# Conv block and attention: the gate, pointwise and feed-forward banks emptied by copies, with silu and GELU applied once over each whole tile

## The chip, the cores and the metric

The kernel runs on one core of one Trainium2 chip. The metric is device time in microseconds. Five engines work on one core, each through its own queue in order: PE (TensorE: matrix products and transposes; its weight loads are shown as PEld), DVE (VectorE), ACT (ScalarE), POOL (GpSimd) and SP (SyncE, which issues DMAs here). [...]

## The reference, cut to what matters

Everything is float32. The input is four pictures of 64 x 64 points with 256 channels. The first layer mixes a small state-space scan, a depthwise convolution and a feed-forward part; the second layer is attention over all 4096 points of a picture.

```python
# layer 1, h = layernorm(x)
x_proj, z = split(h @ in_proj_W)                      # 384 channels each
dt  = silu(proj @ dt_W + dt_b)                        # forward and backward
y_ssm = scan over 2x2 windows with exp(dt * a), 8 states, both directions
y_conv = gelu(depthwise3x3(x_proj) @ pw_W)            # exact GELU
y = alpha * y_ssm + (1 - alpha) * y_conv
x_out = x + (y * silu(z)) @ out_W
fuse = gelu(layernorm(x_out) @ fuse_W1 + fuse_b1) @ fuse_W2 + fuse_b2
x = x_out + fuse
# layer 2
attn = softmax(g @ f.T);  out = gamma * ((attn @ hh) @ Wo + bo) + x
```

## The kernel before, in words

The first layer goes through 32 blocks of 512 points (8 rows of a picture; 8 blocks a picture). Channels stand on the 128 partitions, the 512 points along the row; 384 channels are KI = 3 chunks, the 512 hidden channels of the feed-forward part KF = 4. A generator, `first_layer`, writes out the work of the blocks. `scan(at)` makes the decays (Exp, L406), lets PE turn them into PSUM banks (L462) and lets DVE step the states (L470, L474, L492, L485). Beside it runs `side(at)`, which does the rest of the block before: `conv` (depthwise; products at L574, the other taps on DVE at L595), `gate`, `tail`, and the `head` of the next block. `prepare` makes dt by Silu (L389). Each `yield` names a cost in us, and by these costs the pieces are interleaved.

After the eighth block attention begins. `attend` runs over 128 queries at a time; `weights` makes their scores (L844), copies them out of four banks (L852), takes the maximum on DVE (L858, L860), subtracts it (L877) and takes Exp (L878); L1036 adds up the values. While it runs, `fill(RATE)` draws pieces of the first layer of later pictures. When the first layer is done, `attend_late`, `late_weights` and L1014, L935 do the remaining queries, 256 at a time.

The order so written is the input of a scheduler in the framework, which gives each engine its own list of instructions from its own estimates; a later step puts a table load ahead of each ACT function that the current table doesn't hold. So a program that is built can be listed, engine by engine, and these lists are fixed at run time.

Small products go to PSUM banks from `aside`, a ring of four banks q0 to q3, which the scores use whole (`four`); the scan has a ring of three others (`bank`).

The change touches three places, each of which fills a tile chunk by chunk from such banks:

- `gate`, L342 and L346: three products for z, each emptied by Silu with a bias into a chunk of `zs` (128 x 3 x 512).
- `tail`, L626 and L631: three pointwise products, each emptied by two GELU instructions of 256 columns (they also permute the points) into `yz`. Then, on DVE, L639 and L642 mix in the scan and the gate, and L649 multiplies by out_W; L653 adds the input.
- `tail`, L669 and L673: four products with fuse_W1, each emptied by GELU with a bias into a chunk of `ff` (128 x 4 x 512). L680 multiplies by fuse_W2, L684 adds on DVE. Then come transposes (L312, copied out at L313) and the inputs of attention (L693, L704), stored by SP.

`zs`, `yz` and `ff` have one buffer each; the buffers of `yz` and `ff` are used again in the same block (h2T and vst; ydw and xT).

Of the kernel before, what the change touches and what calls it, by code (L numbers as in the profile page):

```python
# [22 lines left out]
AF = mybir.ActivationFunctionType  # L23
# [11 lines left out]
KI = INNER // P  # L35
# [24 lines left out]
def block_then_attention_kernel(  # L60
# [18 lines left out]
    nc = tc.nc  # L79
# [28 lines left out]
    def load_rows(dst, at):  # L108
        b, i = divmod(at, NBLK)
        for t2 in range(2):  # L110
            for wr in range(ROWS // 2):
                nc.sync.dma_start(
                    out=dst[wr * 32 : (wr + 1) * 32, 2 * t2 : 2 * t2 + 2, :].rearrange("p t c -> p (t c)"),
                    in_=xv[b, i, t2, wr],
                )

    def load_head(at):
        xt = one.tile([P, 4, DIM], F32, tag="norm", name="xt")
        load_rows(xt, at)
        heads[at] = xt  # L120
# [55 lines left out]
    def aside(shape=(P, TOK)):  # L176

        i = turn[0]
        turn[0] = (i + 1) % 4
        return pss.tile(list(shape), F32, tag=f"q{i}", name=f"q{i}")  # L180
# [9 lines left out]
    b_in = wp.tile([P, 2 * KI], F32, name="b_in")  # L190
    b_f1 = wp.tile([P, KF], F32, name="b_f1")
# [98 lines left out]
    def layernorm(dst, src):  # L290

        stats = st.tile([P, 4, 6], F32, tag="stats", name="stats")
        mv = st.tile([P, 4, 2], F32, tag="mv", name="mv")
        for t in range(4):
            nc.vector.bn_stats(stats[:, t, :], src[:, t, :])
        for t in range(4):
            nc.vector.bn_aggr(mv[:, t, :], stats[:, t, :])
        ve = st.tile([P, 4], F32, tag="ve", name="ve")
        rstd = st.tile([P, 4], F32, tag="rstd", name="rstd")
        nc.gpsimd.tensor_scalar(ve, mv[:, :, 1], EPS, None, ALU.add)  # L300
        nc.gpsimd.tensor_tensor(rstd, ve, mhalf, ALU.pow)
        for t in range(4):
            nc.vector.tensor_scalar(
                dst[:, t, :], src[:, t, :], mv[:, t, 0:1], rstd[:, t : t + 1], ALU.subtract, ALU.mult
            )

    def to_channels(dst, src):

        for k in range(KD):
            pt = aside()  # L310
            for t in range(4):
                nc.tensor.transpose(pt[:, t * P : (t + 1) * P], src[:, t, k * P : (k + 1) * P], ident)  # L312
            nc.scalar.copy(dst[:, k, :], pt)  # L313
            yield 0.44
# [21 lines left out]
    def gate(at, whole):  # L336
        xnT = heads[at][0]
        zs = one.tile([P, KI, TOK], F32, tag="zs", name="zs")
        for f in range(KI):
            pz = aside()  # L340
            for k in range(KD):
                nc.tensor.matmul(  # L342
                    pz, lhsT=win[:, k, INNER + f * P : INNER + (f + 1) * P], rhs=xnT[:, k, :],
                    start=(k == 0), stop=(k == KD - 1),
                )
            nc.scalar.activation(zs[:, f, :], pz, AF.Silu, bias=b_in[:, KI + f : KI + f + 1])  # L346
            if not whole:
                yield 1.72
        gates[at] = zs
        if whole:  # L350
            yield 5.2

    def prepare(at):
# [41 lines left out]
        if at < NBLK:  # L395
            yield 3.3
            if at > 0:
                yield from gate(at - 1, True)
# [216 lines left out]
    def tail(at):  # L615

        b, i = divmod(at, NBLK)
        zs, s, ydw = gates.pop(at), heads.pop(at)[1], ydws.pop(at)
        xo = one.tile([P, 4, DIM], F32, tag="xo", name="xo")
        load_rows(xo, at)  # L620

        yz = one.tile([P, KI, TOK], F32, tag="yz", name="yz")
        for f in range(KI):
            pw = aside()
            for k in range(KI):
                nc.tensor.matmul(  # L626
                    pw, lhsT=wpw[:, k, f * P : (f + 1) * P], rhs=ydw[:, k, :],
                    start=(k == 0), stop=(k == KI - 1),
                )
            for t2 in range(2):  # L630
                nc.scalar.activation(  # L631
                    yz[:, f, t2 * 256 : (t2 + 1) * 256].rearrange("p (t1 wr wc) -> p t1 wr wc", t1=2, wr=ROWS // 2),
                    pw.rearrange("p (wr t2 wc t1) -> p t2 t1 wr wc", wr=ROWS // 2, t2=2, t1=2)[:, t2],
                    AF.Gelu,
                )
            yield 2.58

        for f in range(KI):
            nc.vector.scalar_tensor_tensor(  # L639
                yz[:, f, :], yz[:, f, :], one_a[:, f : f + 1], s[:, f, :], ALU.mult, ALU.add  # L640
            )
            nc.vector.tensor_tensor(yz[:, f, :], yz[:, f, :], zs[:, f, :], ALU.mult)  # L642
            yield 1.3
        for t2 in range(2):
            po = aside((P, 2, DIM))
            for t1 in range(2):
                t = 2 * t2 + t1
                for k in range(KI):
                    nc.tensor.matmul(  # L649
                        po[:, t1, :], lhsT=yz[:, k, t * P : (t + 1) * P], rhs=wout[:, k, :],  # L650
                        start=(k == 0), stop=(k == KI - 1),
                    )
            nc.vector.tensor_tensor(xo[:, 2 * t2 : 2 * t2 + 2, :], po, xo[:, 2 * t2 : 2 * t2 + 2, :], ALU.add)  # L653
            yield 3.2

        h2 = one.tile([P, 4, DIM], F32, tag="norm", name="h2")
        layernorm(h2, xo)
        yield 5.0
        for t in range(4):
            nc.gpsimd.tensor_tensor(xo[:, t, :], xo[:, t, :], row, ALU.add)  # L660
        h2T = one.tile([P, KD, TOK], F32, tag="yz", name="h2T")
        yield from to_channels(h2T, h2)
        if at + 3 < LAST:
            load_head(at + 3)
        ff = one.tile([P, KF, TOK], F32, tag="ff", name="ff")
        for f in range(KF):
            pf = aside()
            for k in range(KD):
                nc.tensor.matmul(  # L669
                    pf, lhsT=wf1[:, k, f * P : (f + 1) * P], rhs=h2T[:, k, :],  # L670
                    start=(k == 0), stop=(k == KD - 1),
                )
            nc.scalar.activation(ff[:, f, :], pf, AF.Gelu, bias=b_f1[:, f : f + 1])  # L673
            yield 1.72
        for t2 in range(2):
            pq = aside((P, 2, DIM))
            for t1 in range(2):
                t = 2 * t2 + t1
                for k in range(KF):
                    nc.tensor.matmul(  # L680
                        pq[:, t1, :], lhsT=ff[:, k, t * P : (t + 1) * P], rhs=wf2[:, k, :],
                        start=(k == 0), stop=(k == KF - 1),
                    )
            nc.vector.tensor_tensor(xo[:, 2 * t2 : 2 * t2 + 2, :], pq, xo[:, 2 * t2 : 2 * t2 + 2, :], ALU.add)  # L684
            yield 4.0
        nc.sync.dma_start(out=x1d[at], in_=xo.rearrange("p t c -> p (t c)"))
        yield 0.0

        xT = one.tile([P, KD, TOK], F32, tag="ff", name="xT")
        yield from to_channels(xT, xo)  # L690
        pf = aside()
        for k in range(KD):
            nc.tensor.matmul(pf, lhsT=wfg[:, k, :], rhs=xT[:, k, :], start=(k == 0), stop=(k == KD - 1))  # L693
        fg = two.tile([P, TOK], F32, tag="uT", name="fg")
        nc.scalar.activation(fg, pf, AF.Identity, bias=b_fg)
        nc.sync.dma_start(out=fgd[at], in_=fg)
        yield 1.72

        vst = one.tile([P, 4, DIM + 1], F32, tag="yz", name="vst")
        nc.gpsimd.memset(vst[:, :, DIM : DIM + 1], 1.0)  # L700
        for t in range(4):
            po = aside()
            for k in range(KD):
                nc.tensor.matmul(  # L704
                    po[:, :DIM], lhsT=xT[:, k, t * P : (t + 1) * P], rhs=wv[:, k, :],
                    start=(k == 0), stop=(k == KD - 1),
                )
            nc.vector.tensor_tensor(vst[:, t, :DIM], po[:, :DIM], bv, ALU.add)
            yield 1.2
        nc.sync.dma_start(out=vod[at], in_=vst.rearrange("p t c -> p (t c)"))  # L710
# [35 lines left out]
    def first_layer():  # L746
# [44 lines left out]
        yield from drain("tail", LAST - 2)  # L791
        yield from conv(LAST - 1)
        yield from gate(LAST - 1, False)
        yield from tail(LAST - 1)
        ready["tail"] = LAST - 1

# [392 lines left out]
```

## Time and profile before

| | us |
|---|---|
| median of 3 runs (5250.38 to 5259.54) | 5259.01 |
| the profiled execution's own time | 5265.47 |
| its span | 5263.6 |
| PE busy | 4955.8 (94%) |
| DVE busy | 4517.3 (86%) |
| ACT busy | 3571.5 (68%) |
| ACT table loads, 643 of 1.283 us | 825 |
| POOL busy | 204.0 (4%) |

The profile is of one execution. Busy shares are averages over three stretches with different limits: up to about 880 us the first layer of the first picture runs alone, up to about 4270 us the first layer of the other pictures runs beside attention, and the rest is attention alone. An engine's idle time is put down to whoever released it: "PE q L844 <- ACT zs L346" says that PE stood before a score product into a bank q until ACT had emptied that bank into zs. PE shown as busy includes the modelled ends of pipelined products; PEld shows the weight loads, which run ahead of them.

### The profile page before, as it was taken

How to read it: one execution, taken by the hardware profiler on the slowest of the kernel's cores; microseconds unless marked ns; L12 is line 12 of the kernel's file. 1: busy time of each engine (PE TensorE's matmuls, PEld its weight loads, DVE VectorE, ACT ScalarE, POOL GpSimd, SP SyncE). 2: the span in 40 equal slices, each digit the busy share in tenths (PEclk: the TensorE clock that was granted, in tenths of full speed). 3: DMA queues.
4: the chain of work that ended last, by engine and by line, in shares of the span. 5: the costliest groups of instructions: out<-in, count | busy, mean ns of one | idle time of the engine just before them, and what ended most of it. 6: DMA issues, size and time to landing. Idle time of an engine off the chain costs nothing. (4 is left out here: it accounts for less than half of the span.)

```text
span 5263.6 us, 76327 instructions
## 1 busy us (share of the span) xinstructions
PE 4955.8 (94%) x27138; PEld 3543.4 (67%) x27138; DVE 4517.3 (86%) x8256; ACT 3571.5 (68%) x5489; POOL 204.0 (4%) x304
## 2 busy tenths in 40 slices
PE   7999998999999999999999999999999999999999
PEld 4565565666666666666666666666666667888887
DVE  7999999999899988998989988898989866666665
ACT  6778778667777767677777767777777635555554
POOL 0000000000000000000000000000000000000000
PEclk8999999999999999999999999999999999999999
DMA  1010011333333333334333333333333344444444
GB/s 48 26 44 19 23 34 34 102 122 115 118 104 119 113 109 115 114 116 118 118 111 106 119 108 111 118 114 118 112 116 104 112 129 146 147 147 147 147 147 139
DMA packets 330284, 554.14 MB, mean 105 GB/s; under 512 B 51504, under 2 KB 85936, under 8 KB 329904
## 3 DMA queue, kind: packets, MB, share of 16 engines
q1 hardware_dynamic: 326384, 545.40, 34.2%
q8 instruction: 214, 3.51, 0.3%
q10 hardware_dynamic: 3520, 3.87, 0.2%
q14 instruction: 166, 1.36, 0.1%
HBM read 490.28 MB, written 58.79 MB: 104 GB/s over the span
## 5 line engine op out<-in xcount | busy, mean ns | idle before, releaser
L1036 PE MATMUL acc<-vt,eq 128*128 128x257 f32 x4736 | 1215.4, 392 | 17.2 <-issue 7.6
L406 ACT ACTIVATE e<-dt,a_sc 128x384 f32<-128x384 f32 x1536 | 853.3, 611 | 272.8 <-PE bank L462 262.5
L1036 PEld LDWEIGHTS acc<-vt,eq 128*128 128x128 f32 x4736 | 875.0, 195 | 234.2 <-issue 107.6
L462 PEld LDWEIGHTS bank<-ident,e 128*128 128x128 f32 x4320 | 521.2, 143 | 319.5 <-issue 113.4
L462 PE MATMUL bank<-ident,e 128*128 128x128 f32 x4320 | 658.9, 279 | 79.1 <-DVE p L474 37.1
L1014 PE MATMUL bank<-vt,eT 128*128 128x257 f32 x2560 | 645.8, 382 | 0.0
L492 DVE SCALAR_TENSOR_TENSOR h<-u,bc,p 128x384 f32<-128x384 f32 x1024 | 613.4, 613 | 0.4
L485 DVE SCALAR_TENSOR_TENSOR y<-h,bc,y 128x384 f32<-128x384 f32 x960 | 589.0, 614 | 3.2 <-ACT y L483 0.4
L474 DVE TENSOR_TENSOR p<-bank,h 128x384 f32<-128x384 f32 x960 | 517.1, 548 | 55.1 <-PE bank L462 54.5
L1014 PEld LDWEIGHTS bank<-vt,eT 128*128 128x128 f32 x2560 | 478.6, 189 | 83.7 <-issue 13.9
L852 ACT COPY eq<-q 128x512 f32<-128x512 f32 x592 | 308.6, 587 | 192.6 <-PE q L844 117.5
L948 DVE TENSOR_TENSOR mx<-mx,eT 128x512 f32<-128x512 f32 x378 | 261.7, 692 | 152.2 <-ACT eT L943 121.3
L878 ACT ACTIVATE eq<-eq 128x1024 f32<-128x1024 f32 x296 | 308.1, 1053 | 103.0 <-DVE eq L877 100.1
L877 DVE TENSOR_TENSOR eq<-eq,nb 128x1024 f32<-128x1024 f32 x296 | 357.4, 1220 | 7.6 <-ACT nb L873 7.4
L595 DVE SCALAR_TENSOR_TENSOR ydw<-xp,vec,ydw 128x512 f32<-128x512 f32 x496 | 357.8, 743 | 1.4
L943 ACT COPY eT<-q 128x512 f32<-128x512 f32 x432 | 221.5, 597 | 194.7 <-PE q L935 194.7
L860 DVE TENSOR_TENSOR mx<-mx,eq 128x512 f32<-128x512 f32 x444 | 306.5, 690 | 38.4 <-ACT eq L852 31.5
L406 ACT ACT_TABLE_LOAD x241 | 309.2, 1283 | 14.4 <-PE bank L462 10.2
L485 DVE SCALAR_TENSOR_TENSOR y<-p,bc,y 128x384 f32<-128x384 f32 x512 | 313.1, 612 | 0.4
L470 DVE SCALAR_TENSOR_TENSOR p<-bank,bc,u 128x384 f32<-128x384 f32 x480 | 291.6, 608 | 21.1 <-PE bank L462 20.6
L973 DVE TENSOR_TENSOR eT<-eT,m 128x1024 f32<-128x1024 f32 x216 | 247.7, 1219 | 42.3 <-ACT m L970 42.3
L626 PE MATMUL q<-ydw,wpw 128*128 128x512 f32 x576 | 269.5, 602 | 13.3 <-ACT eq L852 12.8
(154 smaller groups left out, 7524.7 us busy)
## 6 DMA issues: line engine op xcount, KB each, us to landing
vt<-vod SPq DMA_DIRECT2D x1616, 257.0 KB, 2.8
vod<-vst SPq DMA_DIRECT2D x32, 514.0 KB, 3.9
xt<-in_x_dram SPq DMA_DIRECT2D x256, 64.0 KB, 1.9
xo<-in_x_dram SPq DMA_DIRECT2D x256, 64.0 KB, 2.3
x1d<-xo SPq DMA_DIRECT2D x32, 512.0 KB, 2.9
res<-x1d SPq DMA_DIRECT2D x74, 128.0 KB, 2.6
out_dram<-res SPq DMA_DIRECT2D x296, 32.0 KB, 1.6
fgd<-fg SPq DMA_DIRECT2D x32, 256.0 KB, 2.1
```

What stands on the lines that cost most here:

```text
L406: nc.scalar.activation(e[:, f, :], dts[d][:, f, lo : lo + 3 * P], AF.Exp, scale=a_sc[:, d, f * NST + n : f * NST + n + 1],)
L462: nc.tensor.transpose(pa[:, f * P : (f + 1) * P], es[d, n][:, f, off : off + P], ident)
L474: nc.vector.tensor_tensor(p, pa[:, :INNER], hs[d], ALU.mult)
L485: nc.vector.scalar_tensor_tensor(y[:, t, :], h, c, y[:, t, :], ALU.mult, ALU.add)
L492: nc.vector.scalar_tensor_tensor(hs[d], u[d][:, t, :], bc[:, t, d, n : n + 1], p, ALU.mult, ALU.add)
L595: nc.vector.scalar_tensor_tensor(o, x_tap, w_tap, o, ALU.mult, ALU.add)
L852: nc.scalar.copy(e[:, j, :], pr[2 * a + j])
L860: nc.vector.tensor_tensor(mx, mx, e[:, r % 2, :], ALU.max)
L877: nc.vector.tensor_tensor(e8, e8, nb.unsqueeze(1).broadcast_to([P, 8, P]), ALU.add)
L878: nc.scalar.activation(e, e, AF.Exp)
L1014: nc.tensor.matmul(sums[c][:, : DIM + 1], lhsT=e[:, r % 2, s, c * P : (c + 1) * P], rhs=vt[:, s, :], start=(n == 0 and s == 0), stop=(n == ...
L1036: nc.tensor.matmul(acc[:, : DIM + 1], lhsT=es[k // 2][:, k % 2, a : a + P], rhs=vt[:, s, :], start=(n == 0 and s == 0), stop=(n == 2 * NI ...
```

## The change

Each bank is emptied by a copy: Identity with the same bias (zs, ff) or Copy with the same permutation (yz). When the tile is full, one instruction applies Silu or GELU in place over the whole tile: 1536 elements a partition for zs and yz, 2048 for ff. In `gate`, when it runs piece by piece, the wide Silu stands after the last piece's yield; in `tail` the wide GELU stands after the last yield of its loop. The other activations (dt at L389, the Exps) stay as they are. From L349 on, lines move down by one, from L638 by two, from L677 by three.

```diff
@@ gate
-            nc.scalar.activation(zs[:, f, :], pz, AF.Silu, bias=b_in[:, KI + f : KI + f + 1])
+            nc.scalar.activation(zs[:, f, :], pz, AF.Identity, bias=b_in[:, KI + f : KI + f + 1])
             if not whole:
                 yield 1.72
+        nc.scalar.activation(zs, zs, AF.Silu)
         gates[at] = zs
@@ tail
                 nc.scalar.activation(
                     yz[:, f, t2 * 256 : (t2 + 1) * 256].rearrange("p (t1 wr wc) -> p t1 wr wc", t1=2, wr=ROWS // 2),
                     pw.rearrange("p (wr t2 wc t1) -> p t2 t1 wr wc", wr=ROWS // 2, t2=2, t1=2)[:, t2],
-                    AF.Gelu,
+                    AF.Copy,
                 )
             yield 2.58
+        nc.scalar.activation(yz, yz, AF.Gelu)
@@ tail
-            nc.scalar.activation(ff[:, f, :], pf, AF.Gelu, bias=b_f1[:, f : f + 1])
+            nc.scalar.activation(ff[:, f, :], pf, AF.Identity, bias=b_f1[:, f : f + 1])
             yield 1.72
+        nc.scalar.activation(ff, ff, AF.Gelu)
         for t2 in range(2):
```

## The prediction

> **What bounds the kernel now.** I read the busy shares first, then the three stretches of the span, then who waits for whom in the middle one, then the ACT groups. The page's busy line, and the stretches "first layer alone" (0 to 880 us), "first layer beside attention" (to 4270), a short end of it, and "attention alone" (columns: PE, PEld, DVE, ACT, POOL busy us, then clock, DMA share, GB/s):
>
> ```profile
> PE 4955.8 (94%) x27138; PEld 3543.4 (67%) x27138; DVE 4517.3 (86%) x8256; ACT 3571.5 (68%) x5489; POOL 204.0 (4%) x304
> ...
> 0.00:880.00 880.00, 812.58 (x3508) 500.14 (x3508) 830.25 (x1704) 662.88 (x1059) 55.15 (x87) 0.97 0.10 32
> 880.00:4270.00 3390.00, 3162.15 (x17983) 2251.29 (x17983) 3066.38 (x5661) 2422.52 (x3716) 144.59 (x210) 0.97 0.37 113
> 4270.00:4345.00 75.00, 69.95 (x348) 48.95 (x347) 35.17 (x58) 32.46 (x48) 4.29 (x7) 0.98 0.43 128
> 4345.00:5263.00 918.00, 911.13 (x5304) 743.01 (x5302) 585.46 (x836) 453.62 (x669) 0.00 (x0) 1.00 0.49 146
> ```
>
> ACT is the engine that the change touches, and it is never the fullest. Alone, the first layer is paced by DVE (830 of 880 us; 244 of 250 between 250 and 500 us). Beside attention PE is busy 93% and DVE 90% and each waits for the other; ACT is busy 71%. The last 918 us hold none of the changed lines. So at most the idle time that ACT causes on PE and DVE before 4270 us can be won. The lists of waits of the middle stretch, PE's, PEld's and DVE's (us in total, times, longest):
>
> ```profile
> PE q L342 <- ACT eq L852: 20.8, 14, 2.7
> PE q L626 <- ACT eq L852: 12.8, 8, 2.2
> ...
> PE q L844 <- ACT zs L346: 8.2, 10, 2.5
> ...
> PE q L844 <- ACT yz L631: 5.2, 6, 1.6
> ...
> PE q L844 <- ACT ff L673: 1.2, 4, 0.5
> ```
> ```profile
> PEld q L844 <- ACT zs L346: 19.6, 24, 2.7
> ...
> PEld q L844 <- ACT yz L631: 11.2, 19, 1.8
> ```
> ```profile
> DVE mx L860 <- ACT eq L852: 29.4, 28, 2.1
> ...
> DVE mx L858 <- ACT eq L852: 19.5, 18, 2.4
> ...
> DVE yz L639 <- ACT yz L631: 3.7, 3, 2.6
> ```
>
> Adding the whole lists by releaser: ACT ends 105 us of PE idle (75.5 of it the score copies L852, 14.6 the three banks zs, yz, ff) and 60 us of DVE idle (49 of it L852). DVE ends 108 us of PE idle, PE 198 us of DVE idle. Last, what ACT does at the changed lines:
>
> ```profile
> L406 ACT ACT_TABLE_LOAD x241 | 309.2, 1283 | 14.4 <-PE bank L462 10.2
> ...
> L631 ACT ACT_TABLE_LOAD x86 | 110.3, 1283 | 28.0 <-issue 21.5 <-PE q L626 5.5
> L673 ACT ACT_TABLE_LOAD x83 | 106.5, 1283 | 1.4
> ...
> L346 ACT ACT_TABLE_LOAD x79 | 101.4, 1283 | 1.3
> L878 ACT ACT_TABLE_LOAD x77 | 98.8, 1283 | 2.1 <-DVE eq L877 0.9
> L389 ACT ACT_TABLE_LOAD x75 | 96.2, 1283 | 1.3
> ```
>
> With two at the start these are 643 loads, 825 us: 23% of ACT's busy time, most of them because a silu or a GELU stands between two groups of Exp.
>
> **What the Trainium skill says.** All from the page "ScalarE: Activation LUTs". "Table sets: the hidden batching unit" says that copy and identity are in every set. The trace agrees: L331, L423 and L852 (Identity and copies) have no load row. "Step-by-step: what each stage is for" says that time per element does not depend on the function: L331 (Identity, bias) takes 685 ns, L346 (Silu, bias) 687, both 128x512. "What ACT_TABLE_LOAD costs" gives 1283 ns a load plus a drain of about 1380. The load is 1283 here too; of the drain I see nothing: at 431.99 us an Exp ends, at 432.01 the load starts, it ends at 433.29 and the GELU starts at 433.30. I price a load at 1.28 us.
>
> **The change part by part.**
>
> Copies for functions: 96 Silu, 192 GELU of 256 columns and 128 GELU of 512 become Identity or Copy. By the 685/687 pair this costs nothing on ACT, within 35 ns for the 192 Copies (L563, a Copy, takes 721 against 685): at most 7 us of ACT time, which has 29% of slack.
>
> Loads removed: in the built order of the changed program I count 346 loads instead of 643. The three lines keep 32 each (one per block, at the wide instruction), the Exp lines fall from 241 to 141 (L406) and from 77 to 31 (L878), dt goes from 75 to 76. 297 x 1.283 = 381 us less on ACT. Beside attention a block of 141 us has 21.6 loads before and 10.9 after; alone it has 16 and 10.
>
> Wide instructions added: the 128x1024 Exp L878 takes 1053 ns; less 1024 x 0.833 ns (that page's price per element) 200 ns are fixed. So 1536 elements take about 1.48 us (64 of them, zs and yz) and 2048 about 1.91 us (32, ff): 95 + 61 = 156 us. Net on ACT: -381 + 156 = **-225 us**, 8.8 us of a block's 101 beside attention, 2.8 us alone.
>
> What of it reaches the span. *Alone*: nothing; DVE has 2.4% idle there, and 3 us of it is ACT's. *Beside attention*: the banks are emptied without a load ahead of the copy. Of the 14.6 us that PE waited for them I take 10. L852's copies are late when ACT comes from a load, but not when all four ring banks are simply full: four copies of 0.59 us need 2.3 us whatever happens, and ACT itself stood waiting for the scores in 86 of 148 groups (49 times for L844, 37 for L1036), so it was on time there. I take a third of 75.5 us on PE, 25, and 3 of the 9 us at e and dt. Together **-38 us** on PE; the bounds are 0 and 105. DVE's third of 49 us lies inside this, since the two run in step.
>
> What is made later. The first product of fuse_W2 (L680, after: L683) needs the whole ff: last copy 0.69, load 1.28, GELU 1.91, 3.9 us in all, where before the last bank alone was awaited (0.69, and 1.28 if a load stood there). Nothing of ff is ready earlier, so the early products cannot be slipped in. Between the last product into ff and the first out of it the built order puts other PE work: I summed it with issue intervals of the timeline (0.43 us for 512 columns, 0.215 for 257, 0.135 for a 128-column transpose). Beside attention it was 2.2 us a block and becomes 3.1: most often two groups of L462 transposes, L327 x2 and L1036 x4, 2.5 us. In 19 of the 24 blocks beside attention it is short, 24 us in sum. For yz the need is copies 0.7, load 1.28, GELU 1.48 and three DVE steps, 5.6 us; the PE work in between is 2.8 before and 4.0 after; short by 37 us in sum, against 23 us before (need 3.4: the last bank 0.66, a load, two DVE steps). Of those 23 the trace shows 3.5 us as PE idle and 10.2 as PEld idle at L649: the rest is hidden, since PE comes to such places late. Taking these shares, 15 to 45%, of 24 + 37 - 23 = 38 us gives +6 to **+17**; I take 12. DVE's own wait is covered: its first step on yz, L639, was placed level with the transposes that precede the last product, and is now two or more p steps later, about 3.4 us, what the wide GELU needs. In the alone stretch PE's work in between is paced by DVE, so the wait costs nothing there. If that cover failed, it would be 1 to 2 us a block.
>
> zs is used later than it is made; its wide Silu delays only what is queued behind it on ACT (4.0 us with its loads, against 3.3 for one bank with its loads before). PE's score products then wait at most this 0.8 us a block more, 19 us in the worst case, priced in the range. DMAs, POOL and SP keep their instructions; the x1d, fgd and vod writes come a few us later in a block that is used a picture later, so nothing waits.
>
> Sum: -38 + 12 = **-26 us**. On the profiled execution (span 5263.6, its time 5265.47) that gives 5239; the median of the runs, 5259.01, is 6.5 us lower, so I forecast **5233 us**. About 0.2%, 10.5 us, is what a measurement can tell from no change.
>
> **Rivals.** *Slower: the gathered GELU stalls PE.* In-order PE stands at L683 and at the yz products behind a load and 1.9 or 1.5 us of GELU that no built order hides, since the order does not know the load. It decides if PE arrives on time rather than late: then the shortfall of 38 us is paid in full, with up to 19 us from ACT's longer blocks, and the gain falls to the 10 us of the banks plus some 10 of L852: 5259 + 38 + 10 - 20 = about 5285. For it: less ACT delay makes PE earlier, so the hiding shrinks. Against: 3.5 us of 23 was visible before.
> *Nothing: ACT is not the bound.* DVE and PE wait for each other (108 and 198 us) and take the freed time back: 5259, give or take 10.
> *Far faster.* ACT's backlog is behind nearly all of the 105 us on PE, and part of what PE makes DVE wait for (L684 behind L680, 58 us): 5160 to 5190.
> *The loads don't go.* The built order excludes it.
>
> **How the numbers follow.** Gain as worked out, 5210 to 5247: 0.55. Far faster: 0.10. Nothing: 0.13. Slower: 0.22. So faster 0.65, same 0.13, slower 0.22. The range 5185 to 5280 leaves out the lower half of the far case and the upper half of the slow one.
>
> **What would show it.** Right: ACT busy near 3345 us with 346 loads; the waits of L844 for zs, yz and ff gone; L852 releasing some 50 us of PE idle instead of 75; L683 waiting for the wide ff with 5 to 15 us in sum. Wrong: over 25 us at L683 and L651 for ff and yz (slower rival); or ACT's releases halved while DVE's 108 us on PE grow as much (nothing); or DVE in the alone stretch waiting for yz by over 1 us a block.

## The result, and the profile after

The changed kernel takes 5283.31 us in the median of 4 runs (5280.97 to 5286.2), the kernel before 5258.53: 1.0051 times as long, with a 95% interval of 1.0039 to 1.0064. It is **slower by 25 us**, where 26 us of gain were forecast. The profiled execution took 5280.97 us.

From the page of the kernel after, the busy line:

```profile
PE 4960.2 (94%) x27138; PEld 3542.4 (67%) x27138; DVE 4518.3 (86%) x8256; ACT 3332.3 (63%) x5288; POOL 208.2 (4%) x304
```

ACT lost 239 us of busy time (forecast 225); PE's and DVE's busy time stayed. The groups of the loads and of the wide instructions:

```profile
L407 ACT ACT_TABLE_LOAD x141 | 180.9, 1283 | 2.4
...
L677 ACT ACTIVATE ff<-ff 128x2048 f32<-128x2048 f32 x32 | 61.2, 1912 | 0.4
...
L638 ACT ACTIVATE yz<-yz 128x1536 f32<-128x1536 f32 x32 | 47.5, 1485 | 0.4
```

Counts and durations are those of the forecast (1.91 us for ff, 1.48 for yz, and for zs as for yz). So the question is where the time was lost. The first score product (L844, after: L847) starts at 867.9 us before and at 893.9 after; the first product of attention alone at 4359.7 and 4376.8. Cut at these points, the two stretches after are (us, then PE, PEld, DVE, ACT, POOL busy):

```profile
0.00:893.90 893.90, 809.71 (x3442) 499.27 (x3442) 822.24 (x1687) 622.91 (x1018) 58.97 (x89) 0.96 0.10 31
893.90:4376.80 3482.90, 3254.57 (x18475) 2311.27 (x18474) 3122.42 (x5753) 2263.02 (x3614) 149.21 (x215) 0.98 0.38 114
```

The first layer **alone is 26.0 us longer**, the stretch beside attention 8.9 us shorter (3491.8 before). All of the loss lies where "nothing" was forecast. The gain beside attention is no more than the difference between executions: the profiled one of before took 7 us more than the median of its runs, that of after 2 us less.

Alone, the blocks repeat themselves, so one block can be laid beside another, from one copy of proj (L361, after: L362) to the next. A block before, and two blocks after:

```profile
294.58:389.34 94.76, 90.64 (x398) 56.02 (x397) 92.67 (x188) 73.74 (x119) 6.15 (x9) 1.00 0.10 32
```
```profile
499.83:597.67 97.84, 91.15 (x398) 56.08 (x397) 93.08 (x188) 70.56 (x115) 6.56 (x9) 1.00 0.08 25
399.73:499.83 100.10, 93.70 (x398) 58.15 (x397) 93.06 (x188) 70.54 (x115) 6.55 (x9) 0.97 0.08 28
```

Before, a block takes 94.75 us each time. After, it takes 97.84 where TensorE's granted clock is 1.00, and up to 100.1 where short dips of the clock bring its mean down to 0.97. What DVE waits for in the block of 97.84 us:

```profile
DVE h L303 <- POOL rstd L301: 1.2, 1, 1.2
DVE xt L303 <- POOL rstd L301: 1.2, 1, 1.2
DVE p L475 <- PE bank L463: 0.6, 1, 0.6
DVE p L471 <- PE bank L463: 0.5, 1, 0.5
DVE xo L687 <- PE q L683: 0.4, 1, 0.4
DVE vst L711 <- PE q L707: 0.4, 1, 0.4
DVE y L486 <- ACT y L484: 0.2, 1, 0.2
```

Before, the same list has three lines and 1.7 us: the first one here, 0.3 at L708 and 0.2 at L419. After it is 4.5 us. The second line is the largest new one, and it isn't about a changed tile: in the head's layernorm, POOL makes 1/sigma. DVE's order around it after, with the idle time in brackets:

```profile
311.69 0.24 DVE L297 BATCH_NORM_AGGREGATE mv<-stats 128x2 f32<-128x6 f32 x2
311.85 0.72 DVE L596 SCALAR_TENSOR_TENSOR ydw<-xp,vec,ydw 128x512 f32<-128x512 f32 x1
313.81 0.41 DVE L303 TENSOR_SCALAR xt<-xt,mv,rstd 128x256 f32<-128x256 f32 x1 [1.24 <-POOL rstd L301]
```

One row (one DVE instruction) stands between the last aggregate and the normalise that needs POOL's answer. Before, eleven rows stand there (L470 to L485, from 316.88 to 323.05), and there is no wait:

```profile
316.72 0.24 DVE L297 BATCH_NORM_AGGREGATE mv<-stats 128x2 f32<-128x6 f32 x2
...
323.05 0.41 DVE L303 TENSOR_SCALAR xt<-xt,mv,rstd 128x256 f32<-128x256 f32 x1
```

So the built order is another one here, though no instruction of the head was edited. (The expectations below say nine rows: they count lines of the view, two of which hold two rows.)

In the whole stretch DVE's idle time grew by 22 us and its busy time by 4. By releaser the idle time is: 7.4 us more for POOL at xt; 6.6 more for transposed decays (L471, L475); 9.2 more at the two adds behind the products with yz and ff (L655, L687). Other waits fell by a little over 1 us.

Beside attention, PE's waits that the forecast named, after:

```profile
PE q L342 <- ACT eq L855: 17.2, 11, 2.7
...
PE q L651 <- DVE yz L644: 10.0, 10, 2.4
...
PE q L847 <- ACT yz L632: 3.1, 2, 1.5
...
PE q L847 <- ACT zs L346: 2.1, 4, 0.9
```

All that ACT releases on PE there fell from 105.5 to 80.3 us, L852's share (after: L855) from 75.7 to 61.7. What DVE releases rose from 114 to 129 us, and 10.0 us of that are a wait that the list of before doesn't have: the products with yz (L651). In all, PE's waits fell by 8 us, from 230.7 to 222.8.

### The profile page after: what moved, and what is told of

Its sections match the earlier page's. It is cut to its first block, busy times and chain, and to the rows that moved or that the text cites. A ratio compares the mean times of both kernels' runs of the same rounds, so it can differ in the third digit from the quotient of the medians.

```text
span 5279.1 us, 75983 instructions
## 1 busy us (share of the span) xinstructions
PE 4960.2 (94%) x27138; PEld 3542.4 (67%) x27138; DVE 4518.3 (86%) x8256; ACT 3332.3 (63%) x5288; POOL 208.2 (4%) x304
## 5 line engine op out<-in xcount | busy, mean ns | idle before, releaser
L475 DVE TENSOR_TENSOR p<-bank,h 128x384 f32<-128x384 f32 x960 | 516.7, 547 | 47.9 <-PE bank L463 47.2
L855 ACT COPY eq<-q 128x512 f32<-128x512 f32 x592 | 309.4, 590 | 220.9 <-PE q L847 141.5
L471 DVE SCALAR_TENSOR_TENSOR p<-bank,bc,u 128x384 f32<-128x384 f32 x480 | 291.5, 607 | 23.5 <-PE bank L463 23.1
L1017 PE MATMUL acc<-vt,eT 128*128 128x257 f32 x896 | 272.2, 386 | 0.0
```

Source lines behind the costliest of these rows:

```text
L475: nc.vector.tensor_tensor(p, pa[:, :INNER], hs[d], ALU.mult)
L855: nc.scalar.copy(e[:, j, :], pr[2 * a + j])
L1017: nc.tensor.matmul(sums[c][:, : DIM + 1], lhsT=e[:, r % 2, s, c * P : (c + 1) * P], rhs=vt[:, s, :], start=(n == 0 and s == 0), stop=(n == ...
```

## The experiments

Times are medians; the ratio to the kernel before, run on the same chip, stands with its interval. "Alone" is the time until the first score product and "beside" the time from there to attention alone, both from one profile of each kernel (runs of the kernel before alone lie 16 us apart, so small differences between these columns prove nothing). "Block" is the period of a block alone, or the range of six periods where it varies by over 1 us.

| kernel | us | ratio | alone | beside | block |
|---|---|---|---|---|---|
| before | 5258.53 | | 867.9 | 3491.8 | 94.75 |
| after | 5283.31 | 1.0051 (1.0039 to 1.0064) | 893.9 | 3482.9 | 97.84 to 100.13 |
| zs only | 5235.44 | 0.9950 (0.9935 to 0.9965) | 863.5 | 3463.3 | 94.70 |
| yz only | 5301.06 | 1.0077 (1.0062 to 1.0092) | 887.7 | 3509.1 | 96.95 to 99.29 |
| ff only | 5281.17 | 1.0038 (1.0023 to 1.0052) | 887.4 | 3488.1 | 97.69 to 99.39 |
| as before alone, as after beside | 5258.04 | 0.9998 (0.9989 to 1.0006) | 865.6 | 3488.4 | 94.76 |
| after, functions left out | 5229.01 | 0.9944 (0.9929 to 0.9958) | 876.0 | 3450.4 | 95.45 |
| before, functions left out | 5193.85 | 0.9873 (0.9857 to 0.9890) | 862.6 | 3429.3 | 94.22 |
| after, head without POOL's answer | 5281.86 | 1.0044 (1.0029 to 1.0059) | 885.5 | 3491.0 | 96.74 to 98.97 |
| zs, and ff beside only | 5241.24 | 0.9966 (0.9953 to 0.9979) | 864.6 | 3473.5 | 94.70 |
| ff in halves | 5260.21 | 1.0005 (0.9996 to 1.0014) | 879.1 | 3475.9 | 96.46 |
| zs, ff in halves | 5242.04 | 0.9969 (0.9957 to 0.9981) | 875.9 | 3460.6 | 96.40 |
| yz only, GELU left out | 5268.81 | 1.0023 (1.0013 to 1.0033) | 869.4 | 3496.5 | 95.56 |

**The parts one by one.** Each kernel takes one of the three edits of the diff and leaves the others. *zs only*:

```diff
-            nc.scalar.activation(zs[:, f, :], pz, AF.Silu, bias=...)
+            nc.scalar.activation(zs[:, f, :], pz, AF.Identity, bias=...)
...
+        nc.scalar.activation(zs, zs, AF.Silu)
```

> Only gate is changed (copies into zs, one wide Silu); yz and ff as before; 545 loads. In the profiles a block of the first layer alone takes 94.75 us before and 98.9 after, and this makes the whole loss. Theory 'late results' (yz and ff come later than the work that DVE and PE have in between): zs is not urgent, so a block alone stays at 94.8 to 95.8 us, and the kernel takes 5245 to 5262. Rival 'long ACT stops' (any wide instruction between two loads holds up the Exps behind it): a third of the loss, 96 us a block, about 5267. Rival 'the scheduler's order' (any edit gives a new order of about equal badness): 97 to 99 us a block, about 5280.

Measured: 94.70 us a block, and 26 us faster in all (5261.33 for before in these runs). "Late results" foresaw the block; the total is better than it foresaw. The list of DVE's waits in a block is that of before, with the same three times (1.2, 0.3 and 0.2 us). So a wide instruction between two loads need not do harm, and an edit need not bring a bad order.

Where do the 26 us come from? The stretch beside attention, first before, then with the gate edit:

```profile
867.90:4359.70 3491.80, 3255.81 (x18476) 2315.50 (x18475) 3125.37 (x5761) 2468.51 (x3785) 148.88 (x217) 0.98 0.37 113
863.50:4326.80 3463.30, 3227.03 (x18475) 2295.64 (x18474) 3123.84 (x5761) 2383.27 (x3718) 150.55 (x217) 0.98 0.38 114
```

The stretch is 28.5 us shorter, and PE's busy time (first number behind the comma) is 28.8 us shorter for the same products; PE's waits are the same, 230.7 and 231.2 us in sum. By the clock records of the two traces the mean granted clock in this stretch was 0.975 before and 0.984 here, and 3255.8 x 0.975 / 0.984 is about 3226. So in these profiles the gain beside attention is a higher clock and no shorter wait. All four runs of this kernel had a mean clock of 0.983 or 0.984.

*yz only*:

```diff
-                    AF.Gelu,
+                    AF.Copy,
...
+        nc.scalar.activation(yz, yz, AF.Gelu)
```

> Only the pointwise banks are changed (copies into yz, one wide GELU); 540 loads. 'Late results': DVE waits are small at yz but PE's L649 and what follows come later: 95.5 to 97 us a block alone, 5262 to 5275. 'Long ACT stops': 96 us, about 5267. 'Order': 97 to 99 us, about 5280.

Measured: the worst of all, mostly 98.8 to 99.3 us a block and 17 us more beside. A block's window, three of the first four of DVE's waits in it, and what PE waited for most there:

```profile
592.72:691.47 98.75, 93.24 (x398) 58.11 (x397) 93.23 (x188) 69.99 (x115) 6.62 (x9) 0.97 0.08 25
```
```profile
DVE xt L303 <- POOL rstd L301: 1.2, 1, 1.2
...
DVE xo L654 <- PE q L650: 0.9, 1, 0.9
DVE xo L685 <- PE q L681: 0.9, 1, 0.9
```
```profile
PE pa L462 <- ACT e L406: 1.4, 1, 1.4
PE bank L462 <- DVE p L470: 1.2, 1, 1.2
```

The same POOL wait as in the kernel after; 0.9 us at the add behind the products with yz, and 0.9 at the next add, where PE comes late; and a clock of 0.97. The block is what "order" named and longer than "late results" named; the total is above every expectation.

PE does not come late because it waits for yz: no wait for yz stands in its list of this block. It waits 1.4 us for the decays `e`. On ACT a load, the wide GELU and the load back stand in front of that Exp, from 639.56 to 643.65 us, 4.1 us in one piece. (Before, PE's waits for `e` in a block are at most 0.2 us each.) Together with the 1.2 us for DVE just ahead of it, PE was busy 1.17 of the 3.41 us before 643.92; then the clock was 0.50 for the next 3.4 us, in which the products with yz begin. So "long ACT stops", which zs only seemed to exclude, is what the trace shows here, though it had named 96 us: what matters is whether an Exp that PE needs stands behind the stop. The kernel after has the same 1.4 us wait in each of its six regular blocks.

*ff only*:

```diff
-            nc.scalar.activation(ff[:, f, :], pf, AF.Gelu, bias=...)
+            nc.scalar.activation(ff[:, f, :], pf, AF.Identity, bias=...)
...
+        nc.scalar.activation(ff, ff, AF.Gelu)
```

> Only the feed-forward banks are changed (copies into ff, one wide GELU of 2048); 541 loads. In the profile after, DVE waits 1.5 us a block at the add of the fuse_W2 product for PE, which waited for the wide GELU. 'Late results': those 1.5 us or a little more, 96 to 97.5 us a block alone, 5265 to 5278. 'Long ACT stops': 96 us, about 5267. 'Order': 97 to 99 us, about 5280.

Measured: 97.69 us at full clock; DVE waits 1.2 us for POOL at xt, 1.3 for transposed decays and 0.6 at L685. Block and total are those of "order", a little above "late results". The three parts do not add: alone +20 (yz), +19.5 (ff) and -4 (zs), but +26 together. Each of the two slow parts brings the same POOL wait, which is paid once: some 9 us in the stretch, about what the sum is off.

**Where the loss lies.**

```diff
+        if at >= NBLK:
+            nc.scalar.activation(zs, zs, AF.Silu)        # yz and ff in the same way
```

> Blocks 0 to 7 (the first layer alone) as before, blocks 8 to 31 (beside attention) as after. If the loss lies in the alone stretch (+26 us until the first scores in the profiles) and the stretch beside attention gained 9 us: the first scores at 868 us as before, and 5240 to 5255, faster than both. If the loss lies beside attention, or the gain there is only the noise of one profile: 5258 to 5283.

Measured: the first scores at 865.6 us, so the alone stretch is as before, and the total is that of before (0.9998). The loss is the alone stretch. The gain beside is only 3 us in this profile, against 9 after: nothing that can be told from the spread of the runs.

**Load or lateness.**

```diff
-        nc.scalar.activation(yz, yz, AF.Gelu)
+        nc.scalar.activation(yz, yz, AF.Copy)           # Identity for zs and ff
```

> As after, but the three wide instructions apply Identity or Copy: silu and GELU are left out, so that the wide instructions stay as long and as late while their table loads go (154 loads left). At full clock a block alone takes 94.75 us before and about 97.9 after. If the cost is how late the wide results come (0.69 + 1.91 us for ff even without a load), 96 to 97.5 us a block; if the load in front of the wide instruction is what makes it too late, 94.5 to 95.3. Beside attention: shorter than after by 5 to 30 us.

Measured: 95.45 us, between the two ranges and nearer to that of the load. DVE's longest waits in a block of it:

```profile
DVE h L303 <- POOL rstd L301: 1.2, 1, 1.2
DVE xo L687 <- PE q L683: 0.7, 1, 0.7
DVE p L475 <- PE bank L463: 0.6, 1, 0.6
...
```

The POOL wait at xt is gone, since in this built order six rows stand at that place. That is 1.2 of the 2.4 us that a block is shorter than after; PE's wait for `e` is down from 1.4 to 0.5 us. As the order changed with the loads, the two are not taken apart here. Beside attention the stretch is 32 us shorter than after: 23 us less waiting of PE and 9 us less busy time. The other half of the pair takes the functions out of the kernel before:

```diff
-            nc.scalar.activation(ff[:, f, :], pf, AF.Gelu, bias=...)
+            nc.scalar.activation(ff[:, f, :], pf, AF.Identity, bias=...)   # zs too; Copy for yz
```

> As before, but the three banks are emptied by Identity or Copy and silu and GELU are left out: no wide instruction, 154 loads. A block alone 94.3 to 94.8 us (DVE paces it, so loads cost nothing there). Beside attention it bounds what all the removed loads could bring: if ACT's backlog mattered as the forecast took it, 40 us or more below before's 3492; if only the granted clock and the order move that stretch, within 20 us of it.

Measured: 94.22 us a block, as expected (DVE paces it; without functions it is 0.5 shorter). Beside, it is 62 us less than before. That stretch, here and with the wide instructions without functions:

```profile
862.60:4291.90 3429.30, 3227.43 (x18478) 2300.36 (x18477) 3120.27 (x5763) 1970.83 (x3398) 152.33 (x217) 0.98 0.38 115
876.00:4326.40 3450.40, 3245.20 (x18475) 2311.24 (x18474) 3120.74 (x5753) 2077.86 (x3470) 149.24 (x215) 0.98 0.38 115
```

Of the 62 us, 28 are shorter PE busy time (3255.8 to 3227.4, the clock again) and 34 are shorter waits of PE (230.7 to 197.0): somewhat less than the 40 us that the forecast's view of ACT's backlog asked for. Between the two kernels without functions a block alone differs by 1.2 us (95.45 and 94.22). Beside, they differ by 21 us, but 18 of these are PE busy time, and PE's waits are 199.6 and 197.0 us. So wide instructions without loads cost PE next to no waiting there. The kernel after has 192 loads more than these two, and there PE waits 23 us more than with wide instructions without functions, 21 of them behind ACT. So it is the loads that are left, and not the wide instructions as such, that go with the small gain.

**The wait for POOL.**

```diff
-                dst[:, t, :], src[:, t, :], mv[:, t, 0:1], rstd[:, t : t + 1], ALU.subtract, ALU.mult
+                dst[:, t, :], src[:, t, :], mv[:, t, 0:1],
+                mv[:, t, 1:2] if dst is src else rstd[:, t : t + 1], ALU.subtract, ALU.mult
```

> As after, but the head's layernorm multiplies by the variance in place of the 1/sigma that POOL makes: DVE no longer waits for POOL there. Before, nine DVE rows stood between the last aggregate and the first normalise and hid POOL's 1.25 us; after, one row does. If that new order is a part of the loss of its own: 1.2 us less a block alone (96.6 at full clock), 8 to 10 us less until the first scores. If the wait only takes the place of another one: no change, 97.9.

Measured: 96.74 us at full clock, 1.1 less than after, and the first scores 8.4 us sooner. The wait is a part of the loss of its own. The total hardly moved (5281.86): in the profile the stretch beside attention is 8 us longer, 5 of it PE busy time and 2 PE's waits (222.8 to 225.2). The granted clock of these runs was 0.976 to 0.978, against 0.978 and 0.979 for after; why this order gets a lower clock is open.

**ff in halves.**

```diff
-        nc.scalar.activation(ff, ff, AF.Gelu)
+        for t2 in range(2):
+            h = slice(t2 * 256, (t2 + 1) * 256)
+            nc.scalar.activation(ff[:, :, h], ff[:, :, h], AF.Gelu)
```

> As the ff-only kernel (97.69 us a block alone at full clock), but the GELU runs over ff in two halves of 256 points, one behind the other with one load: the first products of fuse_W2 need the first half alone, about 0.85 us earlier, and in the built order six DVE rows, no longer one, stand between the head's aggregate and its normalise. If lateness and the uncovered POOL wait make the price of ff: 94.9 to 96.0 us a block alone, 5250 to 5266. If not: 97 to 98, about 5280.

Measured: 96.46, half a us above the range. The 1.2 us saved are as much as the POOL wait, which is covered in this order. Of the 1.3 us at the transposed decays 1.1 stay, and the earlier half of ff shows only 0.2 us (0.6 to 0.4 at the add). So in this block the late result is the smaller part of ff's price.

**yz without its GELU.**

```diff
-        nc.scalar.activation(yz, yz, AF.Gelu)
+        nc.scalar.activation(yz, yz, AF.Copy)
```

> As the yz-only kernel (98.8 us a block alone, +40 us in all), but the wide instruction is a Copy: GELU on yz is left out, so it is as wide but without loads. The built order still has one DVE row between the head's aggregate and normalise. If load and lateness at yz make its price: 96 us a block alone (the POOL wait of 1.25 stays), and 5245 to 5265. If the price is the order, and the lower clock that comes with it (0.975): 97.5 to 99 us a block, 5280 to 5300.

Measured: 95.56 us a block, 32 us less in all than yz with GELU, though 4 us above the range. A block of it:

```profile
485.33:580.88 95.55, 91.32 (x398) 56.23 (x397) 92.45 (x188) 66.86 (x113) 6.55 (x9) 1.00 0.09 26
```

The POOL wait of 1.2 us is still in its list, so it does not hang on the load: one row stands at that place in this order too. The other 3.2 us a block go with the load: PE's wait for `e` falls from 1.4 to 0.5 us, the two waits of 0.9 at the adds to 0.2 in sum, and the clock is 1.00 again. The order of PE's work changed too, and its share in this is not known.

**What might be better.**

```diff
+        if at >= NBLK:                                   # with zs as after, for all blocks
+            nc.scalar.activation(ff, ff, AF.Gelu)
```

> gate as after; ff as after from block 8 on only; yz as before; 461 loads. From the parts: alone 863.5 us to the first scores as with gate only, beside attention 3463 less the 4 us of ff: 5228 to 5236, faster than before and after. If the gain with gate only is mostly the higher granted clock of its order, this new order may lose it: 5240 to 5262.

Measured: 5241.24, faster than before and after, but 6 us slower than zs only: the parts do not add beside attention either (3473.5 against 3463.3). PE's waits there are 6 us shorter than with zs only and its busy time is 16 us longer, so the second expectation came true, a part of the higher clock lost in a new order.

The other try joins zs with ff in halves, as in the two diffs above.

> gate as after, ff in two halves as in the kernel beside it, yz as before; 445 loads. If parts add: the gate-only kernel's 5235 less what ff's loads bring beside attention (0 to 5 us) plus ff's price alone (0.2 to 1.2 us a block, up to 9 us): 5228 to 5245. If a new order takes the gate's gain: 5250 or more.

Measured: 5242.04. It has the same 96.4 us a block alone as ff in halves, and 3 us less beside than zs only. The best version seen is the gate edit by itself, 5235.44 us.

## Why the prediction was wrong

- **"Alone: nothing" failed**, and with it the sign. The reasoning was that DVE has 2.4% idle there and ACT causes hardly any of it. That bounds a gain. It doesn't bound a loss: DVE had 2.1 us of idle time in a block of 94.76, so hardly any slack in which a new wait could disappear. The block at full clock grew by 3.1 us, of which 2.7 are new idle time of DVE and 0.4 more busy time. With the dips it grew by 4.1 us on average. The forecast had priced it as a branch ("if that cover failed, 1 to 2 us a block") and set it aside.
- What made those 3.1 us was only in small part the waits that the forecast watched. 1.24 us is POOL's 1/sigma in the head, no longer covered. 1.1 us is PE with the transposed decays late, since depthwise products (L575) stand before them in its order, and 0.4 the wide GELU at L683. I had compared the built orders around ff and yz alone; the list of eleven rows against one was there to be read. Over the whole stretch the adds behind the products with yz and ff weigh more: 9.2 of the 26 us.
- **The Exps behind the wide GELU** were left out of the sum for yz. The forecast asked who waits for yz; PE waited for `e`, 1.4 us in each regular block, behind a load, the GELU and a load.
- **DVE's wait on yz** was foreseen as covered, and it was: no line for L641 behind L638 in the block alone, 5.3 us in the whole stretch beside (L639 before: 5.2).
- **-38 us on PE beside attention** was mis-sized. ACT's releases on PE fell by 25 us: 9.4 where scores waited for the banks of zs, yz and ff (10 forecast), 14 at L852 (25 forecast), the rest elsewhere. What DVE releases rose by 14, so that 8 us were left of the 26 forecast.
- **A line was read in the wrong stretch.** The 3.5 us of PE idle time at L649 before, from which the forecast took the visible share of the wait beside attention, all lie in the first layer alone, before the first score product; of the 10.2 us of PEld only 1.3 lie beside. So the line spoke for the stretch where "nothing" was put. The added wait at yz beside attention, 10.0 us against 12 forecast for yz and ff together, is near by luck. (A small one: a 128-column transpose issues every 0.109 us in the trace, not 0.135.)
- **A wrong statement in the slower rival**: the built order does depend on the functions and their loads. Between the last product into ff and L683, PE's work in a block alone takes 4.0 us after and 2.7 without the functions (0.5 before). That hides most of the wait.
- The slower rival named about 5285 us, and 5283 came, by luck. PE did not pay 38 us at L683 and L651 beside attention, but 10. None of the three signs of being wrong that the forecast listed came: the loss was in waits that it did not list.
- The loads removed, the durations, ACT's busy time, and the part of zs (late use, no harm) were right. That zs only gained 26 us, the number forecast for the whole, is luck: the forecast meant shorter waits of PE, and in the profile these did not change.

## What to carry to other kernels

Gathering a table function over a tile costs nothing where the result is used much later (the gate), and costs where the next engine's queue stands right behind it (yz and ff), or where something that another engine needs stands behind it in its own queue (the Exps behind the wide GELU). Before counting the loads saved on an engine with slack, look at the engine that is full: list, in the built order of the changed program, every place where it waits for an answer, and how many of its own rows stand in between, for unchanged tiles too. Try such an edit place by place, since a sum over three places can hide a gain of 0.5% in a loss of 0.5%; and before a gain is put down to a wait, compare the waits and the busy time of the two profiles.

## What the runs showed of the hardware

TensorE's granted clock moved the result and was no part of the forecast. Over the 46 runs of the kernel before that stand beside the experiments, those with a mean clock of 0.978 took 5262 us and those with 0.983 took 5250: about 2.4 us for each 0.001. Between kernels PE's busy time follows the clock more closely: in the thirteen profiles the busy time times the mean clock is 4837 to 4860 us each time. The gate-only kernel got 0.983 to 0.984 in each of its runs, before 0.978 to 0.983, mostly 0.978 to 0.980. By the slope over the runs of before, some 11 of its 26 us would go with that; by the two profiles all of the gain beside attention does. The yz-only kernel got 0.975 each time.

The dips have a pattern. A dip is a stretch in which the clock falls to half, mostly for 3.4 or 6.8 us. Of the 44 dips after 160 us in the profile of before 41 come right after 3.4 us in which PE was busy less than two thirds of the time (45 of 48 for yz only, 27 of 28 for zs only). Fewer than half of such stretches are followed by a dip in before, though (39 of 91, cut at the same phase as the dips). Alone, before has no dip between 160 and 820 us, yz only has one or two in each block, the one at 643.92 behind the waits shown above, and the same program without its GELU has them no more. So the sum of PE's waits, which before and zs only share, does not decide; how they are bunched and where they fall seems to, but no run tests that, and why the gate edit brings fewer dips was not found.
